# An edge layer regrouped: partitions of four m quarters times 32 channels, sums in 128x32 products, VectorE's second operand in PSUM

## The chip, the cores and the metric

The kernel runs on one NeuronCore of a Trainium2 chip. The metric is the device time of one execution in microseconds (us), as the median of several runs. One further execution was recorded by the hardware profiler. All times inside the kernel come from that one.

The engines are called by the profile's names: PE is TensorE (PEld its weight loads), DVE is VectorE, ACT is ScalarE, POOL is GpSimd and SP is the engine that issues most DMAs. SBUF is the working memory and PSUM the memory that PE writes to, in eight banks of 512 float32 values in each of 128 partitions.

## The reference

The input x has shape (4, 56, 56, 128). Four layers are computed, each as `x = x + layer(groupnorm(x))`: a windowed attention layer, an edge layer, a spectral attention layer and a convolution. The change lies in the second one only:

```
# x: (b, l, n, f), all of 4 images, 56 rows l, 56 columns n, 128 channels f
W1, W2 = We[:, :f], We[:, f:]
proj_i = einsum('blnf,of->blno', x, W1)
proj_j = einsum('blnf,of->blno', x, W2)
edge = relu(proj_i[:, :, :, None, :] + proj_j[:, :, None, :, :] + be)
edge_sum = edge.sum(axis=3)                       # over the 56 columns m of the same row
node_in = concatenate([x, edge_sum], axis=-1)
node = relu(einsum('blnc,oc->blno', node_in, Wn) + bn)
```

For every row l and every pair of columns (n, m) of that row there is a relu over 128 channels, summed over m. That is 56 x 56 x 56 x 128 relu terms for an image.

## The kernel before, in words

**Around the edge layer.** `build` treats the four images in turn (`first_layers`): a fast form of the windowed layer (lines below L1140), then `edge_layer` (L1150), then a store. In the measured runs, the branch `small` is taken. Only when the edge layer of the fourth image has ended do the spectra, the attention and the outputs of the later layers begin. The first work of the next stage (POOL's memsets at L339, VectorE's normalization at L193) follows the last `finish` of the edge layer, because its pools take over the space.

**How the edge layer is tiled.** Channels lie on the 128 partitions. An image's 3136 pixels are cut into NBLK = 7 blocks of NB = 448 pixels, that is 8 rows of 56. For one block j:

- `project(j)` (L1181): two products of 128x128 with 448 columns, `pc` = W2 x (L1184) and `pa` = W1 x (L1186), each into a PSUM bank.
- `evacuate(j)` (L1189): ScalarE writes c = -(pc + be) to SBUF (L1194), copies pa to a (L1196), and adds bn to x in place (L1197).
- The relu of a + pc + be is written as max(a, c) - c. Fourteen turns, given by the string `EDGE_TURNS = "ddpddpdpddpddp"` (L1147), handle four values of m each. In a "d" turn (nine of them) VectorE computes max(pa, c) for 4 x 448 values per partition into a tile `e_td` (L1231). It reads pa from PSUM, repeated four times, and c from SBUF, repeated along n. In a "p" turn (five) GpSimd computes a - c into `e_tp` (L1233) and ScalarE applies relu to it in place (L1235).
- After each turn PE sums (L1238): 16 products of a 32x32 identity block with 32 channels of one m. Output partitions are the quarter q of the m, banks are the channel group r, so `acc` has four banks, in which (q, channel of r) are the partitions.
- The correction for the "d" turns is the sum of c over their m, `e_rest`, by one VectorE reduction (L1248).
- At the end of the block ScalarE copies the four banks of acc to `e_sums` (L1250, 128x1792). Then `output` of the block before (L1200) makes six products of 448 columns into the bank `po`: one of x (L1202), one of rest (L1203) and four of sums (L1206). `project(j + 2)` follows.
- `finish(j - 2, po)` (L1211), called in turn 3 of the next block, is one VectorE instruction that takes po from PSUM, applies the last relu and adds to x.

**What sets the order.** Inside `tc.manual_schedule` the instructions of PE, ScalarE and VectorE run in the order in which the Python loop writes them. GpSimd's queue holds only the "p" turns here. Semaphores tie the engines together. A turn's tile comes from a pool of seven ("d") or four ("p"), so VectorE may run up to seven "d" tiles ahead of PE. All eight PSUM banks are used: acc 4, pa 2, and pc and po share 2.

Of the kernel before, what the change touches and what calls it, by code (L numbers as in the profile page):

```python
# [19 lines left out]
P = 128  # L20
# [1129 lines left out]
def edge_layer(k, w, x1, st):  # L1150

    nc, tc = k.nc, k.tc
    xf = x1.rearrange("p l n -> p (l n)")
    nd = 4 * EDGE_TURNS.count("d")
    quarters = [slice(32 * q, 32 * q + 32) for q in range(4)]
    with ExitStack() as es:  # L1160
        big = es.enter_context(tc.tile_pool(name="e_big", bufs=1))
        wk = es.enter_context(tc.tile_pool(name="e_wk", bufs=2))
        psum = es.enter_context(tc.tile_pool(name="e_ps", bufs=2, space=PSUM))

        def bank():
            return psum.tile([P, 512], F32, tag="mm", name="e_mm")

        mr = group_norm_factors(k, wk, bank, st)
        xg = big.tile([P, TOK], F32, name="e_xg")
        shift = wk.tile([P, 1], F32, name="e_shift", bufs=1)  # L1170
        nc.vector.tensor_scalar(shift, mr[:, 0:1], mr[:, 1:2], -1.0, ALU.mult, ALU.mult)
        ready = {}

        def normed(j):
            if j < 2:
                apply_norm(k, xg[:, blk(j)], xf[:, blk(j)], mr)
            elif j < NBLK:
                nc.scalar.activation(xg[:, blk(j)], xf[:, blk(j)], AF.Identity, bias=shift, scale=mr[:, 1:2])

        def project(j):  # L1180
            if j >= NBLK:  # L1181
                return
            pc = psum.tile([P, 512], F32, tag="mm", name="e_pc")
            nc.tensor.matmul(pc[:, :NB], w.W2, xg[:, blk(j)], start=True, stop=True)  # L1184
            pa = psum.tile([P, 512], F32, tag="pa", name="e_pa")
            nc.tensor.matmul(pa[:, :NB], w.W1, xg[:, blk(j)], start=True, stop=True)  # L1186
            ready[j] = pa, pc

        def evacuate(j):  # L1189
            if j >= NBLK:  # L1190
                return
            pa, pc = ready[j]
            c = wk.tile([P, 8, HH], F32, name="e_c")
            nc.scalar.activation(c.rearrange("p l m -> p (l m)"), pc[:, :NB], AF.Identity, bias=w.nbe, scale=-1.0)  # L1194
            a = wk.tile([P, NB], F32, name="e_a")
            nc.scalar.copy(a, pa[:, :NB])  # L1196
            nc.scalar.activation(xf[:, blk(j)], xf[:, blk(j)], AF.Identity, bias=w.bn)  # L1197
            ready[j] = pa, a, c

        def output(j, rest, sums):  # L1200
            po = psum.tile([P, 512], F32, tag="mm", name="e_po")
            nc.tensor.matmul(po[:, :NB], w.Wn[:, 0, :], xg[:, blk(j)], start=True, stop=False)  # L1202
            nc.tensor.matmul(po[:, :NB].rearrange("p (l n) -> p l n", l=8), w.nWn, bc(rest, 2, HH),  # L1203
                             start=False, stop=False)
            for r in range(4):
                nc.tensor.matmul(po[:, :NB], w.Wnq[:, r, :], sums[:, r, :], start=False, stop=(r == 3))  # L1206
            return po

        def finish(j, po):

            nc.vector.scalar_tensor_tensor(xf[:, blk(j)], po[:, :NB], w.nbn, xf[:, blk(j)], ALU.max, ALU.add)  # L1211

        with tc.manual_schedule(engines={mybir.EngineType.PE, mybir.EngineType.Activation, mybir.EngineType.DVE}):
            for j in range(2):
                normed(j)
            for j in range(2):
                project(j)
                evacuate(j)
            last = po = None
            for j in range(NBLK):  # L1220
                pa, a, c = ready.pop(j)
                acc = psum.tile([P, 4, 512], F32, name="e_acc", bufs=1)
                rest = wk.tile([P, 8], F32, name="e_rest")
                at = {"d": 0, "p": nd}
                for g, e in enumerate(EDGE_TURNS):
                    t = wk.tile([P, 4, 8, HH], F32, tag="e_" + e, name="e_t" + e, bufs=7 if e == "d" else 4)
                    cm = bc(c[:, :, at[e]:at[e] + 4].rearrange("p l m -> p m l"), 3, HH)
                    at[e] += 4
                    if e == "d":
                        am = bc(pa[:, :NB].rearrange("p (l n) -> p l n", l=8), 1, 4)  # L1230
                        nc.vector.tensor_tensor(t, am, cm, ALU.max)  # L1231
                    else:
                        nc.gpsimd.tensor_sub(t, bc(a.rearrange("p (l n) -> p l n", l=8), 1, 4), cm)  # L1233
                        tf = t.rearrange("p m l n -> p (m l n)")
                        nc.scalar.activation(tf, tf, AF.Relu)  # L1235
                    for q in range(4):
                        for r, o in enumerate(quarters):
                            nc.tensor.matmul(acc[quarters[q], r, :NB], k.ident[o, o],  # L1238
                                             t[o, q].rearrange("p l n -> p (l n)"),
                                             start=(g == 0), stop=(g == len(EDGE_TURNS) - 1))  # L1240
                    if g == 3 and po is not None:
                        finish(j - 2, po)
                    if g == 5 and j:
                        evacuate(j + 1)
                    if g == 8:
                        normed(j + 2)
                    if g == 9:
                        nc.vector.tensor_reduce(rest, c[:, :, 0:nd], AX.X, ALU.add)  # L1248
                sums = wk.tile([P, 4, NB], F32, name="e_sums")
                nc.scalar.copy(sums, acc[:, :, :NB])  # L1250
                if last:
                    po = output(*last)
                project(j + 2)
                last = j, rest, sums
            finish(NBLK - 2, po)
            finish(NBLK - 1, output(*last))


def edge_weights(k, w, pool):

    for n, t in (("nbe", w.be), ("nbn", w.bn), ("nWn", w.Wn[:, 1, :])):
        r = pool.tile(list(t.shape), F32, name="e_" + n)
        k.nc.vector.tensor_scalar_mul(r, t, -1.0)
        setattr(w, n, r)


def l1_host(i):
    We, Wn = i["L1_conv_We"], i["L1_conv_Wn"]
    W2 = Wn[:, P:].T.reshape(4, 1, 32, P)
    return {  # L1270
        "w1_W1": We[:, :P].T, "w1_W2": We[:, P:].T, "w1_be": i["L1_conv_be"].reshape(P, 1),
        "w1_Wn": Wn.T.reshape(2, P, P).transpose(1, 0, 2), "w1_bn": i["L1_conv_bn"].reshape(P, 1),
        "w1_Wnq": np.broadcast_to(W2, (4, 4, 32, P)).reshape(4, P, P).transpose(1, 0, 2),
    }


# [1564 lines left out]
```

## Time and profile before

| what | value |
|---|---|
| time, median of 3 runs | 3583.2 us (3579.53 to 3584.5) |
| the profiled execution's own time | 3579.81 us |
| its span, first to last instruction | 3578.0 us |
| mean granted TensorE clock | 0.981 |
| PE busy, share of the span | 3372.0 us, 94% |
| DVE busy | 2702.3 us, 76% |
| ACT busy | 2089.9 us, 58% |
| POOL busy | 1249.2 us, 35% |
| edge layer of the four images, from its first normalization to its last finish | 150.46, 150.50, 150.50 and 150.70 us |

A page of the profile gives the busy time of each engine, the groups of instructions (source line, engine, operation, tile written and tiles read, shapes, count, busy time and mean duration), and the chain of work that ended last. The shares above are means over stages that have different limits, so what one stage is worth is read from that stage alone. Two views serve for this: the table of engine busy times in chosen windows, and the timeline, which merges neighbouring instructions of one kind and shows in brackets how long an engine sat idle before them and what it waited for. A PE product in float32 is recorded as two weight loads and two matmul instructions, so counts of PE instructions are twice the products in the code. Ends of matmuls are modelled: a run of them is better read from start to start.

### The profile page before, as it was taken

The numbers are of one execution on the slowest core, as the hardware profiler recorded it, in microseconds if no ns is written. First come the engines' busy times: TensorE is split into PE (matmuls) and PEld (weight loads), VectorE is DVE, ScalarE is ACT, GpSimd is POOL, SyncE is SP. The second block draws the span as 40 slices with busy tenths as digits, with TensorE's granted clock in tenths as the row PEclk, the third lists the DMA queues.
The fourth block names the chain that finished last, engine by engine and source line by source line (L and its number), as shares of the span: only waits on it lengthen the run. The fifth ranks groups of instructions, "written<-read, shape, count | busy, mean of one in ns | idle before, by whom it ended". The sixth has DMA issues, their size and how long they took to land.

```text
span 3578.0 us, 80873 instructions
## 1 busy us (share of the span) xinstructions
PE 3372.0 (94%) x36096; PEld 1549.4 (43%) x36096; DVE 2702.3 (76%) x2531; ACT 2089.9 (58%) x2103; POOL 1249.2 (35%) x752
## 2 busy tenths in 40 slices
PE   6999998989999898999999999999898899999998
PEld 4433344553333455333344643333456443336664
DVE  6588868767888696688859758887784678886776
ACT  4688865458888564688856458887552112214442
POOL 1000017600000581000018400000673778884686
PEclk8999999999999999999999999999998999999999
DMA  2144420014333000444310024442103027763101
GB/s 103 43 92 92 95 42 20 20 47 94 88 88 83 20 3 20 99 93 94 89 44 3 20 57 94 94 94 63 38 3 101 15 53 178 181 148 91 55 19 55
DMA packets 98076, 244.51 MB, mean 68 GB/s; under 512 B 64456, under 2 KB 69832, under 8 KB 92712
## 3 DMA queue, kind: packets, MB, share of 16 engines
q0 software_dynamic: 16128, 102.77, 14.2%
q1 hardware_dynamic: 74872, 123.64, 11.9%
q10 hardware_dynamic: 6720, 12.85, 1.3%
q8 instruction: 285, 4.67, 0.5%
q14 instruction: 71, 0.58, 0.1%
HBM read 79.46 MB, written 31.33 MB: 31 GB/s over the span
## 4 chain that ended last, share of the span: by engine, by line
PE 79%; DVE 10%; ACT 4%; issue 4%; POOL 3%; DMA 0%; POOLq 0%; DVEq 0%; ACTq 0%
PE f_pm L818 17%; PE f_pm L684 15%; PE u_po L1878 8%; PE e_acc L1238 7%; PE q_acc L1732 3%; DVE e_td L1231 3%; PE f_pm L791 2%; PE e_po L1206 2%; PE f_pm L770 2%; ACT f_ring L821 1%; PE f_pm L464 1%; PE o_d L2141 1%; DVE f_acc L673 1%; PE o_d L2538 1%; PE f_pm L715 1%
## 5 line engine op out<-in xcount | busy, mean ns | idle before, releaser
L821 ACT ACTIVATE f_ring<-f_pm 128x1792 f32<-128x1792 f32 (+1 forms) x764 | 1093.8, 1482 | 228.7 <-PE f_pm L818 181.2
L673 DVE TENSOR_TENSOR f_acc<-f_acc,f_ring 128x1792 f32<-128x1792 f32 x468 | 947.7, 2025 | 191.1 <-ACT f_ring L821 160.9
L818 PE MATMUL f_pm<-f_qT,f_kT 32*128 32x448 f32 x5376 | 725.2, 571 | 15.5 <-ACT f_ring L821 5.1
L684 PE MATMUL f_pm<-f_ring,f_va 128*32 128x448 f32 (+1 forms) x6304 | 589.4, 490 | 0.0
L663 POOL DMA_DIRECT2D f_far<-f_ring x112 | 96.6, 862 | 1329.3 <-ACT f_ring L821 1108.2
L1231 DVE TENSOR_TENSOR e_td<-e_pa,e_c 128x1792 f32<-128x1792 f32 x252 | 491.2, 2018 | 14.1 <-ACT e_a L1196 14.1
L1233 POOL TENSOR_TENSOR e_tp<-e_a,e_c 128x1792 f32<-128x1792 f32 x140 | 451.5, 3261 | 101.4 <-PE e_acc L1238 59.8
L818 PEld LDWEIGHTS f_pm<-f_qT,f_kT 32*128 32x128 f32 x5376 | 260.4, 183 | 417.2 <-ACT f_ring L821 304.7
L1238 PE MATMUL e_acc<-e_td,t_shared 32*32 32x448 f32 x8064 | 325.8, 545 | 24.9 <-DVE e_td L1231 24.0
L684 PEld LDWEIGHTS f_pm<-f_ring,f_va 128*32 128x32 f32 x6304 | 164.2, 109 | 409.7 <-issue 397.4
L1873 DVE TENSOR_TENSOR u_ud<-u_px,u_d 112x1792 f32<-112x1792 f32 x144 | 263.5, 1864 | 39.6 <-PE u_po L1878 35.4
L1235 ACT ACTIVATE e_tp<-e_tp 128x1792 f32<-128x1792 f32 x140 | 233.4, 1694 | 74.0 <-POOL e_tp L1233 74.0
L1875 POOL TENSOR_TENSOR u_up<-xh,u_d 112x1792 f32<-112x1792 f32 (+1 forms) x72 | 240.9, 3376 | 55.0 <-PE u_po L1878 39.7
L1238 PE MATMUL e_acc<-e_tp,t_shared 32*32 32x448 f32 x4480 | 222.6, 544 | 3.0 <-ACT e_tp L1235 2.4
L1878 PE MATMUL u_po<-u_ud,AT 112*64 112x448 f32 x1056 | 213.8, 544 | 1.9 <-DVE u_ud L1873 1.9
L1238 PEld LDWEIGHTS e_acc<-e_td,t_shared 32*32 32x32 f32 x8064 | 142.3, 103 | 138.4 <-DVE e_td L1231 79.4
L1878 PEld LDWEIGHTS u_po<-u_ud,AT 112*64 112x64 f32 x1056 | 74.4, 138 | 128.8 <-issue 112.9
L1250 ACT COPY e_sums<-e_acc 128x1792 f32<-128x1792 f32 x28 | 46.3, 1652 | 136.2 <-PE e_acc L1238 136.2
L1238 PEld LDWEIGHTS e_acc<-e_tp,t_shared 32*32 32x32 f32 x4480 | 96.5, 103 | 53.0 <-issue 16.6
L728 DVE RECIPROCAL f_den<-f_den 128x448 f32<-128x448 f32 x28 | 82.6, 2951 | 44.1 <-ACT f_den L725 44.1
L1717 POOL TENSOR_TENSOR q_u<-iS,q_g 128x1792 f32<-128x1792 f32 x32 | 102.8, 3236 | 23.0 <-PE q_acc L1732 22.8
L1732 PE MATMUL q_acc<-q_u,S 64*64 64x448 f32 x1024 | 104.6, 553 | 4.4 <-DVE q_u L1719 3.3
(525 smaller groups left out, 4511.6 us busy)
## 6 DMA issues: line engine op xcount, KB each, us to landing
f_far<-f_ring POOLq DMA_DIRECT2D x112, 896.0 KB, 6.3
u_d<-dd SPq DMA_DIRECT2D x46, 784.0 KB
f_far<-f_ring SPq DMA_DIRECT2D x28, 896.0 KB
xw<-in_x SPq DMA_DIRECT2D x4, 1568.0 KB
x2d<-x SPq DMA_DIRECT2D x4, 1568.0 KB
xat<-x SPq DMA_DIRECT2D x4, 1568.0 KB
x_xs<-xat ACTq DMA_DIRECT2D x32, 196.0 KB
xm<-x_ev ACTq DMA_DIRECT2D x64, 98.0 KB
```

Source lines behind the costliest of these rows:

```text
L673: nc.vector.tensor_add(e.acc, e.acc, slots(j, c))
L684: nc.tensor.matmul(e.po[heads[h], part], va[o, c, heads[h]], p, start=(c == 0), stop=(c == 23 and part.stop == NB))
L818: nc.tensor.matmul(ss[:, i, :NB], kT[heads[h], c * P:(c + 1) * P], qT[heads[h], blk(j)], start=True, stop=True)
L821: nc.scalar.activation(ring[:, slot:slot + m, :], ss[:, :m, :NB], AF.Exp, scale=scale)
L1231: nc.vector.tensor_tensor(t, am, cm, ALU.max)
L1233: nc.gpsimd.tensor_sub(t, bc(a.rearrange("p (l n) -> p l n", l=8), 1, 4), cm)
L1235: nc.scalar.activation(tf, tf, AF.Relu)
L1238: nc.tensor.matmul(acc[quarters[q], r, :NB], k.ident[o, o], t[o, q].rearrange("p l n -> p (l n)"), start=(g == 0), stop=(g == len(EDGE_TUR ...
L1732: nc.tensor.matmul(acc[bp][i][halves[hb % 2], hb // 2, :NB], x[o], u[o, 8 * hb:8 * hb + 8, :].rearrange("p h t -> p (h t)"), start=first, ...
L1873: nc.vector.tensor_mul(u, bc(px[:, :, :NB], 2, m), dm)
L1875: nc.gpsimd.tensor_mul(u, bc(x, 2, m), dm)
L1878: nc.tensor.matmul(po[64 * b2:64 * b2 + 64, :NB], st.AT[:, 8 * i + h0 + q, 2 * bp + b2, :], u[:, b2, q, :], start=(left == 16), stop=(left ...
```

## The change

Instead of the 128 channels of one m at a time, a tile now carries, on its partitions, four quarters of the m (m = 14 q + i) times 32 channels, and, along its free axis, the four channel groups r. A turn handles the four m values with the same i.

- `project` makes four products for pa, one for each r, with the 32 channels of W1 repeated four times (weights from the host), into four single banks. For pc it makes 16 products of 128x32 with 112 columns, with -W2, which put the 14 m values of a quarter q into partition range q.
- `evacuate` is split in two parts, after turns 5 and 7. ScalarE moves the four pa banks to SBUF, with be added (`e_a`, 4 x 448), and pc to `e_c`. Block 1's evacuation moves from ahead of the loop into block 0.
- A "d" turn reads `e_a` from SBUF as its first operand and pc from PSUM, repeated along n, as its second. A "p" turn reads `e_a` and `e_c` from SBUF. The tile is 128x1792 as before. In block 0 the first three "d" turns and the first "p" turn are cut into four pieces, one for each r.
- PE sums a turn in four products of 128x32, one for each r, with a stack of four 32x32 identities, into the four partition ranges of one bank `acc`. Partitions of acc are now the channels.
- Four more such products subtract rest (128x4x8 now) inside acc. `e_sums` becomes 128x448, and `output` two products: x and sums.
- Banks: pa 4, pc 2, acc 1, and one for po and the normalization's small products.
- On the host: the packed weights hold W1 four times, a stack of identities and its negative; the four-times-wide Wn for sums and its negated copy go.

`EDGE_TURNS` stays as it is; the new turn letter "s" that the code knows doesn't occur in it. The diff, cut to its core:

```diff
         def project(j):
             if j >= NBLK:
                 return
-            pc = psum.tile([P, 512], F32, tag="mm", name="e_pc")
-            nc.tensor.matmul(pc[:, :NB], w.W2, xg[:, blk(j)], start=True, stop=True)
-            pa = psum.tile([P, 512], F32, tag="pa", name="e_pa")
-            nc.tensor.matmul(pa[:, :NB], w.W1, xg[:, blk(j)], start=True, stop=True)
-            ready[j] = pa, pc
-
-        def evacuate(j):
+            pa = [psum.tile([P, 512], F32, name="e_pa", bufs=4) for r in range(4)]
+            pc = psum.tile([P, 512], F32, name="e_pc", bufs=2)
+
+            def first(r):
+                nc.tensor.matmul(pa[r][:, :NB], w.W1[:, r, :], xg[:, blk(j)], start=True, stop=True)
+            first(0)
+            xm = xg[:, blk(j)].rearrange("p (l m) -> p l m", l=8)
+            for r, o in enumerate(quarters):
+                for q in range(4):
+                    nc.tensor.matmul(pc[quarters[q], 8 * M * r:8 * M * (r + 1)].rearrange("p (l m) -> p l m", l=8),
+                                     w.nW2[:, o], xm[:, :, M * q:M * (q + 1)], start=True, stop=True)
+            for r in range(1, 4):
+                first(r)
...
+        def evacuate(j, part):
...
-            c = wk.tile([P, 8, HH], F32, name="e_c")
-            nc.scalar.activation(c.rearrange("p l m -> p (l m)"), pc[:, :NB], AF.Identity, bias=w.nbe, scale=-1.0)
-            a = wk.tile([P, NB], F32, name="e_a")
-            nc.scalar.copy(a, pa[:, :NB])
-            nc.scalar.activation(xf[:, blk(j)], xf[:, blk(j)], AF.Identity, bias=w.bn)
...
+            for r in range(2 * part, 2 * part + 2):
+                nc.scalar.activation(a[:, r, :], pa[r][:, :NB], AF.Identity, bias=w.be[:, r:r + 1])
+                if r == 0:
+                    nc.scalar.copy(c.rearrange("p r l m -> p (r l m)"), pc[:, :NB])
+            if part == 1:
+                nc.scalar.activation(xf[:, blk(j)], xf[:, blk(j)], AF.Identity, bias=w.bn)
+
+        def terms(j, m, t, r0, r1, e):
+            pc, _, c, a = ready[j]
+            if e == "d":
+                c = pc[:, :NB].rearrange("p (r l m) -> p r l m", r=4, l=8)
+            cm = bc(c[:, r0:r1, :, m], 3, HH)
+            am = a[:, r0:r1, :].rearrange("p r (l n) -> p r l n", l=8)
+            if e == "d":
+                nc.vector.tensor_tensor(t, am, cm, ALU.max)
+            else:
+                nc.gpsimd.tensor_sub(t, am, cm)
+                tf = t.rearrange("p r l n -> p (r l n)")
+                nc.scalar.activation(tf, tf, AF.Relu)
...
             po = psum.tile([P, 512], F32, tag="mm", name="e_po")
             nc.tensor.matmul(po[:, :NB], w.Wn[:, 0, :], xg[:, blk(j)], start=True, stop=False)
-            nc.tensor.matmul(po[:, :NB].rearrange("p (l n) -> p l n", l=8), w.nWn, bc(rest, 2, HH),
-                             start=False, stop=False)
-            for r in range(4):
-                nc.tensor.matmul(po[:, :NB], w.Wnq[:, r, :], sums[:, r, :], start=False, stop=(r == 3))
+            nc.tensor.matmul(po[:, :NB], w.Wn[:, 1, :], sums, start=False, stop=True)
...
-            for j in range(2):
-                project(j)
-                evacuate(j)
+            project(0)
+            for part in range(2):
+                evacuate(0, part)
+            project(1)
...
+                if j == 0:
+                    early = {g: tile_of(EDGE_TURNS[g]) for g in
+                             [g for g, e in enumerate(EDGE_TURNS) if e == "d"][:3] + [EDGE_TURNS.index("p")]}
+                    for r in range(4):
+                        for g, t in early.items():
+                            terms(j, ms[g], t[:, r:r + 1], r, r + 1, EDGE_TURNS[g])
...
-                    for q in range(4):
-                        for r, o in enumerate(quarters):
-                            nc.tensor.matmul(acc[quarters[q], r, :NB], k.ident[o, o],
-                                             t[o, q].rearrange("p l n -> p (l n)"),
-                                             start=(g == 0), stop=(g == len(EDGE_TURNS) - 1))
+                    for t, r0 in parts:
+                        for r in range(t.shape[1]):
+                            nc.tensor.matmul(acc[quarters[r0 + r], :NB], w.S[:, 0, :], t[:, r].rearrange("p l n -> p (l n)"),
+                                             start=(g == 0), stop=False)
                     if g == 3 and po is not None:
                         finish(j - 2, po)
-                    if g == 5 and j:
-                        evacuate(j + 1)
+                    if g == 5:
+                        evacuate(j + 1, 0)
+                    if g == 7:
+                        evacuate(j + 1, 1)
+                    if g == 10:
+                        normed(j + 2)
                     if g == 8:
-                        normed(j + 2)
-                    if g == 9:
-                        nc.vector.tensor_reduce(rest, c[:, :, 0:nd], AX.X, ALU.add)
-                sums = wk.tile([P, 4, NB], F32, name="e_sums")
-                nc.scalar.copy(sums, acc[:, :, :NB])
+                        if ns:
+                            nc.vector.tensor_reduce(rest[:, 0:2], ready[j][2][:, 0:2, :, 0:nd + 1], AX.X, ALU.add)
+                        nc.vector.tensor_reduce(rest[:, 2 if ns else 0:4], ready[j][2][:, 2 if ns else 0:4, :, 0:nd], AX.X, ALU.add)
+                for r in range(4):
+                    nc.tensor.matmul(acc[quarters[r], :NB].rearrange("p (l n) -> p l n", l=8), w.S[:, 1, :],
+                                     bc(rest[:, r, :], 2, HH), start=False, stop=True)
+                sums = wk.tile([P, NB], F32, name="e_sums")
+                nc.scalar.copy(sums, acc[:, :NB])
                 if last:
                     po = output(*last)
                 project(j + 2)
```

## The prediction

> **What bounds the kernel now.** I read the page first, then, for the edge layer alone, the table of engine busy times in windows, the chain of waits, and the timelines of VectorE and PE. The page gives the groups that the edit touches:
>
> ```profile
> L1231 DVE TENSOR_TENSOR e_td<-e_pa,e_c 128x1792 f32<-128x1792 f32 x252 | 491.2, 2018 | 14.1 <-ACT e_a L1196 14.1
> L1233 POOL TENSOR_TENSOR e_tp<-e_a,e_c 128x1792 f32<-128x1792 f32 x140 | 451.5, 3261 | 101.4 <-PE e_acc L1238 59.8
> ```
>
> VectorE's turns (252 = 28 blocks x 9) never wait inside a block; GpSimd waits for PE (to get a tile back). The windows of two successive blocks of the first image, from finish to finish, show why:
>
> ```profile
> core 0: us, PE busy (x) PEld busy (x) DVE busy (x) ACT busy (x) POOL busy (x), PEclk, DMA share, GB/s
> 615.84:635.52 19.68, 19.68 (x465) 11.71 (x464) 18.42 (x12) 12.09 (x11) 16.13 (x6) 1.00 0.01 2
> 635.52:655.20 19.68, 19.68 (x465) 11.70 (x464) 18.42 (x11) 12.09 (x11) 16.14 (x6) 1.00 0.01 3
> ```
>
> The first number is the block's length, then each engine's busy time. PE is busy for all 19.68 us, VectorE for 18.42. The chain of waits over such a block is PE alone:
>
> ```profile
> 597.62 13.47 PE e_acc L1238 x437
> 611.09 0.95 PE e_po L1202 x2
> 612.04 0.75 PE e_po L1203 x2
> 612.79 3.01 PE e_po L1206 x8
> 615.80 0.75 PE e_pc L1184 x2
> 616.55 0.75 PE e_pa L1186 x2
> ```
>
> So 14 turns of sums take 13.47 us, 0.962 a turn, and eight full products of 448 columns 6.21, that is 0.75 each and 0.2 for the change of array mode. VectorE pays for PE at each finish:
>
> ```profile
> 604.84 9.74 DVE L1231 TENSOR_TENSOR e_td<-e_pa,e_c 128x1792 f32<-128x1792 f32 x5
> 615.84 0.69 DVE L1211 SCALAR_TENSOR_TENSOR x<-e_po,e_nbn,x 128x448 f32<-128x448 f32 x1 [1.26 <-PE e_po L1206]
> ...
> 683.57 3.95 DVE L1231 TENSOR_TENSOR e_td<-e_pa,e_c 128x1792 f32<-128x1792 f32 x2
> 694.45 0.68 DVE L1211 SCALAR_TENSOR_TENSOR x<-e_po,e_nbn,x 128x448 f32<-128x448 f32 x1 [6.93 <-PE e_po L1206]
> 699.03 0.68 DVE L1211 SCALAR_TENSOR_TENSOR x<-e_po,e_nbn,x 128x448 f32<-128x448 f32 x1 [3.89 <-PE e_po L1206]
> ```
>
> Blocks 2 to 6 each hold a finish that waits (1.14, then four times 1.26: 6.18 us an image), and after the last VectorE turn (687.52) PE needs another 11.5 us until the last finish starts. From the five turns in 9.74 us with 2.02 for one, turns follow each other every 1.93 to 1.94 us.
>
> **What the Trainium skill says.** "TensorEngine Tiling (Array Packing)", Available Configurations, lists 128x32 as four independent tiles, and Key Properties says that changing the mode drains the engine. The trace agrees: the 0.2 us above, and these lines from the attention of the first layer, where 128x32 products write the four partition ranges of one bank:
>
> ```profile
> 1053.46 0.96 PE L684 MATMUL f_pm<-f_ring,f_va 128*32 128x448 f32 x8
> ...
> 1056.70 0.96 PE L715 MATMUL f_pm<-f_acc,c_ones 128*32 128x448 f32 x8
> ```
>
> Eight instructions (four products) read 0.96; a run of 16 of L684 reads 1.71, so four products take 0.75 in a stream, as one full product does. "VectorE: DVE Perf Modes", The perf-mode tier table, gives float32 tensor_tensor one rate whether operands are in SBUF or PSUM. The trace agrees: 2018 ns with the first operand in PSUM, 2025 (L673) with both in SBUF, 1549 for 1344 elements with the second in PSUM (L761), all about 1.04 ns an element plus 150. "SBUF — State Buffer", Who interferes with whom: a VectorE instruction with at most one SBUF input doesn't contend with GpSimd, one with two does. Before and after have one; before, GpSimd's turns stay within 3245 to 3279 ns beside VectorE. That stands for "after" too, but no line here has the new operand arrangement.
>
> **The change part by part, for a block.**
>
> PE, sums: 14 turns x 0.75 = 10.5 in place of 13.47. PE, output: two products, 1.5, in place of six, 4.5. PE, rest inside acc: four 128x32 products, 0.75 (the product of the spread rest, L1203, ran at 0.75, so repeated columns cost nothing). PE, pa: 4 x 0.75 = 3.0 in place of 0.75. PE, pc: 16 products of 112 columns. If four overlap, 4 x 0.75/4 = 0.75; by the issue pace of the 32x32 turns (0.962/32 = 0.030 an instruction) 32 x 0.030 = 0.96; without any overlap 16 x 0.75/4 = 3.0. I take 0.96, since eight 128x32 instructions overlap in the lines above, and keep 0.75 and 3.0 as ends. Mode changes: four a block (into output, into pc, out of it, into sums) x 0.2 = 0.8. Sum: 10.5 + 1.5 + 0.75 + 3.0 + 0.96 + 0.8 = 17.5 in place of 19.68 (ends 17.3 and 19.6).
>
> VectorE: nine turns x 1.94, a reduction of 288 elements (0.36 start to start) and a finish (0.60): 18.42, unchanged. The turn's cost is the one thing that no row shows in its new form. Lower end: 1792 elements at 1.04 ns are 1.87, 0.07 less a turn; upper end: the accumulating adds of L673 follow each other every 2.13 when they don't wait (three in 6.29), 0.19 more. I take 1.94: two L761 products of 1344 and 448 elements, 1.549 + 0.612 long, take 2.09 together at 1156.74, so an instruction with its second operand in PSUM also overlaps its successor by 0.07.
>
> So VectorE becomes the bound at 18.42, and PE's 0.9 of slack covers its own share. Is finish then free of its wait? After the last turn of a block PE has one or two turns (0.75 each), rest (0.75) and output (1.5) to do: po is there some 4 us after VectorE's last turn. VectorE does three turns (5.8 us) before finish, so the wait goes. PE comes to sums again after project, some 8.5 us in, with four or five of the seven "d" tiles full, so VectorE doesn't stop for a tile either.
>
> ScalarE: five relus x 1.70, evacuation of four pa banks 4 x 0.6, of pc 0.53, x 0.68, xg 0.75, sums 0.53 in place of 1.65: some 13.4, in place of 12.09, within 18.42. Its queue matters at the split evacuation only: part 0 stands behind the relu of turn 5, part 1 behind that of 7, and neither is needed before the next block. If that cover were gone, each microsecond late would delay GpSimd's first tile, which itself is four tiles ahead. GpSimd: 5 x 3.23 = 16.1, unchanged, within 18.42. No DMA is moved; the packed weights are about as large as before.
>
> Start of the image: now the first turn starts 4.4 us after the normalization (549.24 to 553.64). After: pa 0 at the slow early pace (the next product's first instruction at 551.45 follows those two of 549.80 by 1.65, some 0.8 an instruction), to 551.3, pc by 552.9 to 553.4, ScalarE's copy of pc (0.53) until some 553.9: +0.3. The copy and VectorE read the same bank, and the first turn of before likewise started only when ScalarE had left pa's bank (3.48 us idle, until L1196). Then twelve pieces of 448 elements, 0.54 start to start (L729 to L738) = 6.5 in place of three turns, 5.8: +0.7. ScalarE and PE supply pieces every 0.75, less than the 1.6 that VectorE needs for three. Project(1) on PE is over by some 560, when the first tiles are full.
>
> End of the image: from VectorE's last turn, before, 687.52 to 699.71, 12.2. After: one turn's sums 0.75 + 0.14, turn 13 0.75, rest 0.75: 2.4. Output of block 5, 1.5, to 3.9. The one po bank makes output of block 6 wait for finish of 5 (0.69, to 4.9), then 1.5, and finish to 7.35. That is 4.8 less.
>
> Sum for an image: 6.18 + 4.8 - 0.3 - 0.7 = 10.0. Nothing else runs beside the edge layer's end: the next stage's first VectorE and GpSimd work (699.13, 699.63) follows the last finish, after all four images. So 4 x 10.0 = 40 us. Against the profiled execution's own 3579.8 that gives 3539.8; the median of the runs shown stands 3.4 above it, so 3543.
>
> **The rivals.** First: pc doesn't overlap, and PE stays the bound at 19.0 to 19.6. For it: strided reading of 14 columns at a time, of which no row shows a case; against it: L684's pace. Then finish's wait shrinks only by 0.1 to 0.7 in five blocks, the end by 4.8: 4 x (2 + 4.8 - 1.5) = 21: 3562.
>
> Second, slower: VectorE's turns lose their overlap and follow every 2.13. For it: L673's chain, and an operand order not seen before; against it: L761, and that L673 reads its own output. Price: 60 whole turns and 12 pieces an image, 72 x 0.19 = 13.7, x 4 = 55, less 40: 15 slower, 3598. It decides from 40/288 = 0.14 us an instruction. Third: the four sums of a turn don't overlap, against L684 and L715: 14 x 3.0 = 42 us a block, over 800 us slower. Fourth: VectorE's turn gets 0.07 cheaper, with a PE that just follows (17.5): 252 x 0.07 = 18 more: 3525.
>
> **How the numbers follow.** Forecast 0.70 (3534 to 3552), PE still the bound 0.12 (3552 to 3570), VectorE's overlap lost 0.10 (3577 to 3600), cheaper turns 0.05 (3523 to 3534), sums without overlap 0.03. Range 3530 to 3566: it leaves out the last two, the slower case and the rims. About 0.2% (7 us) is what a measurement of this kernel can tell from no change. Faster by more: 0.70 + 0.12 + 0.05 = 0.87, less 0.01 at the rim; same 0.03; slower 0.11.
>
> **What would show it.** Right: in the windows from finish to finish 18.4 us, VectorE busy all of it, PE some 17; no wait for e_po before finish in blocks 2 to 6; the e_td mean at 2018; 56 + 4 sum products a block at 0.75 per four; from last turn to last finish 7 to 8 us; edge layer some 140.5 us in place of 150.5. Wrong: e_td longer than 2.02 or spaced by more than 2.0, VectorE waiting for PE inside a block, pc above 2 us a block, or GpSimd's mean well above 3261.

## The result, and the profile after

| | before | after |
|---|---|---|
| median of the timed runs, us | 3581.8 (4 runs, 3579.5 to 3584.5) | 3539.5 (4 runs, 3534.4 to 3542.2) |
| ratio to before, 95% interval | 1 | 0.988 (0.9863 to 0.9897) |
| profiled execution, its span, us | 3579.8, 3578.0 | 3540.0, 3538.2 |
| edge layers of the four images, us | 150.6, 150.6, 151.5, 150.8: 603.5 | 140.1, 140.0, 140.2, 140.4: 560.8 |
| all the rest of the span, us | 2974.5 | 2977.4 |

An edge layer is counted here from the start of the write of e_shift, VectorE's first instruction after the normalization's statistics, to the end of the last finish, both from VectorE's timeline. (The table of the profile before has 150.50 for the third image; counted as there it is 151.34.) The gain lies there: 42.7 us less in the profiled executions, with 2.9 given back outside. The groups of the page that answer to those of before (the changed kernel has other line numbers):

```profile
L1222 DVE TENSOR_TENSOR e_td<-e_a,e_pc 128x1792 f32<-128x1792 f32 (+1 forms) x288 | 493.3, 1781 | 15.3 <-ACT e_c L1210 15.1
L1224 POOL TENSOR_TENSOR e_tp<-e_a,e_c 128x1792 f32<-128x1792 f32 (+1 forms) x152 | 453.7, 3023 | 75.1 <-issue 43.2
L1277 PE MATMUL e_acc<-e_td,t_edge 128*32 128x448 f32 x2016 | 225.4, 543 | 42.4 <-DVE e_td L1222 42.4
```

The means of 1781 and 3023 ns mix whole turns with pieces of 448 elements; VectorE's busy time in the group, 493.3 us, was 491.2 before. What has turned round is the last line: PE now idles 42.4 us for tiles of VectorE, where before it was busy in the whole block. The windows of two blocks of the first image, from finish to finish, columns as before:

```profile
core 0: us, PE busy (x) PEld busy (x) DVE busy (x) ACT busy (x) POOL busy (x), PEclk, DMA share, GB/s
616.03:634.36 18.33, 17.43 (x172) 6.50 (x164) 18.33 (x12) 12.32 (x14) 16.15 (x6) 1.00 0.00 1
634.36:652.69 18.33, 17.43 (x172) 6.51 (x164) 18.33 (x12) 12.32 (x14) 16.15 (x6) 1.00 0.01 2
```

VectorE is busy for the whole block of 18.33 us, PE for 17.43. The chain of waits over one block, which was PE alone before, now passes from PE to VectorE and back:

```profile
614.53 0.75 PE e_pa L1190 x2
615.28 0.90 PE e_pc L1195 x32
616.19 2.45 PE e_pa L1190 x6
618.64 3.19 PE e_acc L1277 x32
...
622.41 0.23 DVE e_rest L1290
622.64 0.14 issue
622.78 5.88 DVE e_td L1222 x3
628.66 0.04 issue
628.70 1.71 PE e_acc L1277 x16
630.41 0.75 PE e_acc L1292 x8
631.16 0.95 PE e_po L1234 x2
632.11 0.75 PE e_po L1235 x2
```

Four products of the rest take 0.75 (L1292), the output 1.70 in two products with its change of mode, the sixteen products of pc 0.90 (32 instructions), and four sum groups 3.19. VectorE's timeline shows the start, a finish inside the layer and the end:

```profile
555.83 12.26 DVE L1222 TENSOR_TENSOR e_td<-e_a,e_pc 128x448 f32<-128x448 f32 x15 [3.78 <-ACT e_c L1210]
...
616.03 0.68 DVE L1240 SCALAR_TENSOR_TENSOR x<-e_po,e_nbn,x 128x448 f32<-128x448 f32 x1
616.62 5.87 DVE L1222 TENSOR_TENSOR e_td<-e_a,e_pc 128x1792 f32<-128x1792 f32 x3
...
677.78 5.87 DVE L1222 TENSOR_TENSOR e_td<-e_a,e_pc 128x1792 f32<-128x1792 f32 x3
687.90 0.68 DVE L1240 SCALAR_TENSOR_TENSOR x<-e_po,e_nbn,x 128x448 f32<-128x448 f32 x1 [4.26 <-PE e_po L1235]
690.45 0.68 DVE L1240 SCALAR_TENSOR_TENSOR x<-e_po,e_nbn,x 128x448 f32<-128x448 f32 x1 [1.86 <-PE e_po L1235]
```

The finish at 616.03 has no bracket: it waits for nothing, where the finish at the same place waited 1.26 before. From the last turn's end (683.65) to the last finish's end (691.13) are 7.48 us, 12.2 before.

### The profile page after: what moved, and what is told of

It reads as the page before. It is cut to its first block, busy times and chain, and to the rows that moved or that the text cites. A ratio compares the mean times of both kernels' runs of the same rounds, so it can differ in the third digit from the quotient of the medians.

```text
span 3538.2 us, 64217 instructions
## 1 busy us (share of the span) xinstructions
PE 3317.8 (94%) x27696; PEld 1429.6 (40%) x27696; DVE 2694.3 (76%) x2566; ACT 2102.1 (59%) x2199; POOL 1251.9 (35%) x764
## 4 chain that ended last, share of the span: by engine, by line
PE 75%; DVE 15%; ACT 4%; issue 3%; POOL 2%; DMA 0%; DVEq 0%; POOLq 0%; ACTq 0%; SPq 0%
PE f_pm L818 18%; PE f_pm L684 15%; PE u_po L1924 8%; DVE e_td L1222 7%; PE q_acc L1778 3%; PE e_acc L1277 3%; PE f_pm L791 2%; PE f_pm L770 2%; PE e_pa L1190 2%; ACT f_ring L821 1%; PE o_d L2584 1%; PE f_pm L464 1%; PE s_pr L1573 1%; PE o_d L2187 1%; DVE f_acc L673 1%
## 5 line engine op out<-in xcount | busy, mean ns | idle before, releaser
L684 PE MATMUL f_pm<-f_ring,f_va 128*32 128x448 f32 (+1 forms) x6304 | 591.0, 491 | 0.0
L1222 DVE TENSOR_TENSOR e_td<-e_a,e_pc 128x1792 f32<-128x1792 f32 (+1 forms) x288 | 493.3, 1781 | 15.3 <-ACT e_c L1210 15.1
L1224 POOL TENSOR_TENSOR e_tp<-e_a,e_c 128x1792 f32<-128x1792 f32 (+1 forms) x152 | 453.7, 3023 | 75.1 <-issue 43.2
L684 PEld LDWEIGHTS f_pm<-f_ring,f_va 128*32 128x32 f32 x6304 | 163.9, 109 | 410.7 <-issue 398.4
L1277 PE MATMUL e_acc<-e_td,t_edge 128*32 128x448 f32 x2016 | 225.4, 543 | 42.4 <-DVE e_td L1222 42.4
L1226 ACT ACTIVATE e_tp<-e_tp 128x1792 f32<-128x1792 f32 (+1 forms) x152 | 236.9, 1583 | 45.3 <-POOL e_tp L1224 44.9
L1277 PE MATMUL e_acc<-e_tp,t_edge 128*32 128x448 f32 x1120 | 131.0, 540 | 3.3 <-ACT e_tp L1226 3.1
L1277 PEld LDWEIGHTS e_acc<-e_td,t_edge 128*32 128x32 f32 x2016 | 55.5, 109 | 191.0 <-DVE e_td L1222 115.3
L1924 PE MATMUL u_po<-u_up,AT 112*64 112x448 f32 x480 | 103.9, 546 | 2.4 <-POOL u_up L1921 2.4
L1190 PE MATMUL e_pa<-e_xg,t_edge 128*128 128x448 f32 x224 | 101.1, 578 | 5.1 <-DVE e_xg L193 5.1
```

The lines of the kernel that those rows point to most:

```text
L684: nc.tensor.matmul(e.po[heads[h], part], va[o, c, heads[h]], p, start=(c == 0), stop=(c == 23 and part.stop == NB))
L1224: nc.gpsimd.tensor_sub(t, am, cm)
L1277: nc.tensor.matmul(acc[quarters[r0 + r], :NB], w.S[:, 0, :], t[:, r].rearrange("p l n -> p (l n)"), start=(g == 0), stop=False)
L1924: nc.tensor.matmul(po[64 * b2:64 * b2 + 64, :NB], st.AT[:, 8 * i + h0 + q, 2 * bp + b2, :], u[:, b2, q, :], start=(left == 16), stop=(left ...
```

## Experiments

My theory was the prediction's: PE was the bound, the change takes PE below VectorE, and from there VectorE sets the block. Its rivals were that the gain came from elsewhere (VectorE's new operand, the new start), or that PE is still in the way. The table gives each kernel's time and, from its profile, the sum of the four edge layers and one block of the first image. Two kernels with the same code outside the edge layer differ by up to 16.5 us there (half_turn_room and no_pieces), so a difference of a few microseconds is read from the edge layers and not from the total.

| kernel | median us | ratio to before (95%) | edge layers | block | PE, VectorE, GpSimd busy in it |
|---|---|---|---|---|---|
| after | 3539.5 | 0.988 (0.9863 to 0.9897) | 560.8 | 18.33 | 17.43, 18.33, 16.15 |
| after_again | 3544.2 | 0.9888 (0.9873 to 0.9903) | 561.1 | | |
| before_one_sum | 3530.6 | 0.9866 (0.9849 to 0.9882) | 557.9 | 18.33 | 17.66, 18.33, 16.40 |
| both_in_sbuf | 3956.2 | 1.1059 (1.1041 to 1.1078) | 979.8 | 33.30 | 21.99, 33.30, 22.05 |
| pc_serial | 3546.6 | 0.991 (0.9893 to 0.9926) | 567.1 | 18.33 | 18.33, 18.33, 16.03 |
| pe_plus_1 | 3547.4 | 0.9896 (0.9881 to 0.9911) | 560.6 | 18.33 | 18.18, 18.33, 16.14 |
| pe_plus_4 | 3572.7 | 0.9982 (0.9975 to 0.9988) | 590.0 | 20.23 | 20.23, 18.42, 16.16 |
| no_pieces | 3556.1 | 0.9923 (0.9909 to 0.9936) | 569.6 | | |
| last_bank | 3535.3 | 0.9866 (0.9851 to 0.9881) | 556.7 | | |
| half_turn | 3541.1 | 0.9893 (0.9877 to 0.991) | 555.7 | 17.78 | 17.64, 17.53, 17.78 |
| half_turn_and_bank | 3543.6 | 0.9892 (0.9877 to 0.9907) | 552.5 | | |
| spare_products | 3548.2 | 0.9907 (0.9893 to 0.992) | 561.0 | | |
| half_turn_room | 3530.9 | 0.9852 (0.9838 to 0.9865) | 550.5 | 17.79 | 17.64, 17.53, 17.79 |

**Was PE the bound before?** In the kernel before, three of the output's four products with the sums are left out; nothing else of it changes.

```diff
-            for r in range(4):
+            for r in range(3, 4):
                 nc.tensor.matmul(po[:, :NB], w.Wnq[:, r, :], sums[:, r, :], start=False, stop=(r == 3))
```

> The kernel before, with one of the four products of sums in output; three quarters of the edge sums are left out of the result. Theory (PE bounds a block before): PE 19.68 - 3 x 0.75 = 17.43 us a block, below VectorE's 18.42, so the finish no longer waits (6.2 us an image) and the end of an image shrinks by two outputs, 4.5: 4 x 10.7 = 43 less, 3539 us, though nothing else of the change is in. Rival (the gain comes from the new operands or the new order): only the end shrinks, 4 x 4.5 = 18 less, 3564.

Measured: 3530.6 us, and this block:

```profile
613.48:631.81 18.33, 17.66 (x460) 10.06 (x458) 18.33 (x13) 11.87 (x11) 16.40 (x6) 1.00 0.01 3
```

With some 2 us less on PE and VectorE's operands, layout and start untouched, the block falls to the same 18.33 us as in the changed kernel, with VectorE busy in all of it, and the edge layers lose 45.6 us. That is all of the changed kernel's gain in the edge layers and a little more (the start stays as it was). So the gain is PE's relief; the new operands and layout are the way to it.

**What VectorE's second operand in PSUM is worth.** VectorE's turns read e_c, the copy in SBUF that GpSimd reads anyway.

```diff
-            if e == "d":
-                c = pc[:, :NB].rearrange("p (r l m) -> p r l m", r=4, l=8)
```

> The changed kernel, but VectorE's turns take their second operand from the copy of pc in SBUF, so both come from SBUF, beside GpSimd's turns. Theory (two SBUF inputs contend with GpSimd): if they exclude one another, a block takes 17.4 + 16.2 = 33.6 us in place of 18.33, some 430 us more in all; if GpSimd alone is stretched, up to its slack of 2.2 us a block is hidden; I expect at least 3600. Rival (float32 operands cost the same wherever they lie, also beside GpSimd): 3540, e_td at 2.02 and e_tp at 3.26.

Measured: 3956.2 us. The table of one block, and in a second fence the two groups of turns by tile (min/median/max in ns, pieces of 448 elements included, then first and last start):

```profile
639.75:673.05 33.30, 21.99 (x165) 6.54 (x164) 33.30 (x13) 11.91 (x13) 22.05 (x5) 0.74 0.00 0
```

```profile
L1220 DVE TENSOR_TENSOR e_td<-e_a,e_c x288: 610/2014/5084, 555.7 to 3051.4; 128x1792 f32<-128x1792 f32 x120, 128x448 f32<-128x448 f32 x24
L1222 POOL TENSOR_TENSOR e_tp<-e_a,e_c x152: 1202/4641/5172, 555.8 to 3038.2; 128x1792 f32<-128x1792 f32 x136, 128x448 f32<-128x448 f32 x16
```

The turns of the two engines exclude each other. Of VectorE's 240 whole turns, 116 still take 2.0 us, but the other 124 take 4.6 to 5.08, which is nearly one turn of its own (2.02) and one of GpSimd (3.26 when undisturbed), and GpSimd's reach 5.17. (The medians in the fence mix both kinds with the pieces.) The wait for the other engine counts as busy time in the longer instruction, so no idle column shows it: VectorE reads 33.30 us busy out of 33.30 for work of 18.33. The reckoning from full exclusion, 33.6 us a block and 430 more in all, stands against 33.30 and 416.7 measured. The Trainium skill, "SBUF — State Buffer", Who interferes with whom, has the rule (a VectorE instruction with two SBUF inputs contends with a GpSimd instruction that reads SBUF); these runs agree and give the size. GpSimd reads both its operands from SBUF, so the operand in PSUM isn't a detail of the change: without it the change would cost 374 us against before.

**Does the order of the pc products matter?** Two loops exchanged, so that four successive products write the same partition range.

```diff
-            for r, o in enumerate(quarters):
-                for q in range(4):
+            for q in range(4):
+                for r, o in enumerate(quarters):
```

> The changed kernel, with the 16 products of pc in the other order: four successive ones write the same partition range. Theory (the overlap over the four ranges is what makes them cheap): pc takes up to 3.0 us in place of 0.90, PE up to 19.5 us a block, above VectorE's 18.33; five blocks an image longer by 1.2 and the start later by 2: 4 x 8 = 32 more, 3572. Rival (pc runs at the issue pace in any order, 0.03 an instruction): 0.9 to 1.0, 3540.

Measured: 3546.6 us. From the chain and from the table of one block:

```profile
615.14 2.13 PE e_pc L1195 x32
```

```profile
615.77:634.10 18.33, 18.33 (x166) 7.75 (x164) 18.33 (x12) 12.42 (x14) 16.03 (x6) 1.00 0.00 1
```

Neither side was right: the sixteen products take 2.13 us in place of 0.90, so the order counts, but not the 3.0 of a stream without any overlap. PE's 18.33 then just fits VectorE's block, which stays; the 6.3 us more in the edge layers are the starts, where pc is on the path. In the four images the first turn comes 6.9, 5.9, 6.0 and 7.0 us after e_shift, and 4.7 to 4.9 in the changed kernel: 6.6 more in all. The exchange has a second effect that no run separates from the first: four successive products shared their weights before it, and share their columns of x after it.

**How much slack has PE?** A product of the first projections is repeated, once and four times, from the third block of an image on, and writes the same values again.

```diff
+            for n in range(1 if j > 1 else 0):
+                first(3)
```

and with 4 for 1.

> The changed kernel with one product of project made twice, in the five projects inside the blocks (0.75 us of PE each). Theory (0.9 us of slack a block): PE 18.18 a block, still below VectorE's 18.33, nothing is lost, 3540 (at most 3 more). Rival (no slack): 20 x 0.75 = 15 more, 3555.

> The changed kernel with the last product of project made five times instead of once, in the five projects inside the blocks (3.0 us of PE each). Theory (PE has 0.9 us of slack a block): each of those blocks grows by 3.0 - 0.9 = 2.1, 5 x 4 x 2.1 = 42 more, 3581, which is the time before. Rival (no slack, all on the path): 20 x 3.0 = 60 more, 3600.

Measured, one block of each:

```profile
618.13:636.46 18.33, 18.18 (x174) 6.93 (x166) 18.33 (x13) 12.32 (x14) 16.14 (x6) 1.00 0.01 1
```

```profile
615.61:635.84 20.23, 20.23 (x173) 8.16 (x172) 18.42 (x12) 12.44 (x14) 16.16 (x6) 1.00 0.01 2
```

One product (0.75) disappears: block 18.33, edge layers 560.6 against 560.8 (the total's excess over the changed kernel lies outside of them). Four bring the old picture back, PE busy throughout, VectorE at 18.42, and the wait ahead of finish, here in VectorE's timeline:

```profile
635.84 0.68 DVE L1242 SCALAR_TENSOR_TENSOR x<-e_po,e_nbn,x 128x448 f32<-128x448 f32 x1 [1.81 <-PE e_po L1237]
```

The edge layers lose 7.3 us an image, where I had reckoned 10.5. A late block is only 1.90 longer (20.23 less 18.33), not 2.1: PE's own work in the changed kernel is then 20.23 less 3.0, or 17.23, and its slack nearer to 1.1 than to 0.9. And only four blocks of an image pay. Of the five finishes inside the layer of the first image the first doesn't wait at all, the second waits 1.35 and the others 1.81; they stand 19.75 and three times 20.23 apart. The likely reason, not tested by itself, is a lead of the engines that the first late projects use up.

**Do the twelve pieces of the first block earn their place?** The branch for the first block is switched off; its turns are whole and wait for the whole evacuation.

```diff
-                if j == 0:
+                if j < 0:
```

> The changed kernel with whole turns in block 0, too. The first turn then waits for all four evacuations of pa, which ended 2.9 us after the first turn's start in the changed kernel; the twelve pieces took 0.65 more than three whole turns. Theory (VectorE is the bound from its first turn on): 4 x (2.9 - 0.65) = 9 more, 3549. Rival (PE comes late to the first sums anyway, and a later start is hidden): 3540.

Measured: 3556.1 us, edge layers 569.6: 8.8 more, 2.2 an image. VectorE's timeline (e_shift was written at 553.27):

```profile
560.61 11.68 DVE L1222 TENSOR_TENSOR e_td<-e_a,e_pc 128x1792 f32<-128x1792 f32 x6 [6.29 <-ACT e_a L1208]
```

The first turn starts 7.3 us after e_shift, 2.5 later than in the changed kernel, and in the other images 2.2 to 3.9 later: 11.5 in all. Less the 0.65 an image that whole turns save, 8.9 are left, about what the edge layers lost. The four pa banks, PE's 3.0 us in place of 0.75, would lie on the start if the turns weren't cut.

**What limits the changed kernel now: the end and VectorE.** Two edits, each alone. The last output of an image goes to the bank of pc, which nobody uses then:

```diff
-            po = psum.tile([P, 512], F32, tag="mm", name="e_po")
+            po = psum.tile([P, 512], F32, tag="e_pc" if j == NBLK - 1 else "mm", name="e_po",
+                           bufs=2 if j == NBLK - 1 else 1)
```

> The changed kernel, with the last output of an image written to the free bank of pc instead of the one po bank. Theory: its products no longer wait for the finish before (PE sat idle 0.8 to 0.9 us there): 4 x 0.9 = 3.6 less, 3536; from the last turn to the last finish's end 6.6 in place of 7.5. Rival (the copy of sums would hold it anyway): 3540.

Measured: 3535.3 us, the best until then; edge layers 556.7, 1.0 less an image. The two finishes at the end, in VectorE's timeline:

```profile
675.40 5.87 DVE L1222 TENSOR_TENSOR e_td<-e_a,e_pc 128x1792 f32<-128x1792 f32 x3
685.52 0.68 DVE L1241 SCALAR_TENSOR_TENSOR x<-e_po,e_nbn,x 128x448 f32<-128x448 f32 x1 [4.26 <-PE e_po L1236]
687.03 0.68 DVE L1241 SCALAR_TENSOR_TENSOR x<-e_po,e_nbn,x 128x448 f32<-128x448 f32 x1 [0.82 <-PE e_po L1236]
```

They start 1.51 us apart in place of 2.55, and the end takes 6.45 us in place of 7.48. The output of block 6 does wait for the finish of 5 in the changed kernel, as the prediction's sum for the end had it.

The other edit gives half of one of VectorE's turns in a block to GpSimd ("s" is a turn in two halves, one for each):

```diff
-EDGE_TURNS = "ddpddpdpddpddp"
+EDGE_TURNS = "ddpddpspddpddp"
```

> The changed kernel with one of the nine VectorE turns shared: two channel groups on VectorE, two on GpSimd. Theory (VectorE is now the bound, at 18.33, with PE at 17.43 and GpSimd at 16.15): VectorE 17.5, GpSimd 17.9, PE 17.5 with no room; a block takes some 17.9, 28 x 0.43 = 12 less, 3528. Rival (with three engines this near to each other, waits of one for the other eat it): 3540 or more.

Measured: 3541.1 us, one block:

```profile
613.35:631.13 17.78, 17.64 (x165) 6.45 (x164) 17.53 (x12) 13.38 (x15) 17.78 (x7) 1.00 0.00 1
```

GpSimd is the bound at 17.78, with PE 0.14 and VectorE 0.25 behind it. The edge layers gain 5.1 us, not the 12 expected: the end takes 9.28 instead of 7.48, and finish waits again, 1.25 to 2.11 the first time in an image and about 0.26 from then on. And the total gains nothing: the stretch after the fourth edge layer takes 897.3 us in place of 892.0. I put both edits together, to see whether they add up:

> The changed kernel with the shared turn and with the last output in pc's free bank. The shared turn alone made a block 17.78 us (GpSimd busy all of it) and the four edge layers 555.7 in place of 560.8; the bank alone 556.7. Theory: the two add up, edge layers 551.5 to 552, 9 us less than the changed kernel, 3530. Rival (with the shared turn PE is later at the image's end, so that the bank is free in time anyway): 555, 3535.

Measured: 3543.6 us. The edge layers do add up (552.5), the total doesn't: the last stretch is now 902.9. The first difference to look at is the loads of s_x, which the attention stage behind it reads. The same line in the changed kernel:

```profile
2497.24 1.98 SPq L2827 DMA_DIRECT2D s_x<-xad  x4
```

and in half_turn:

```profile
2638.79 2.56 SPq L2827 DMA_DIRECT2D s_x<-xad  x4
```

They go out at 2497 us ahead of the fourth edge layer in the one, and at its very end in the other, where PE then waits 4.89 us for them (5.11 in half_turn_and_bank). That wait is not itself what costs the time: the changed kernel has waits of 2.83 and 2.56 at the same place, and PE gets to the next step (s_ps) 15.9 us after the last finish in half_turn and 17.2 in the changed kernel. half_turn falls behind later, at a VectorE instruction on one element a partition. In half_turn and in the changed kernel:

```profile
2678.33 7.73 DVE L1505 SCALAR_TENSOR_TENSOR s_t<-s_t,s_mv 128x1 f32<-128x1 f32 x1
```

```profile
2689.77 0.23 DVE L1505 SCALAR_TENSOR_TENSOR s_t<-s_t,s_mv 128x1 f32<-128x1 f32 x1
```

PE waits 9.13 us for it in half_turn, 1.83 in the changed kernel. In half_turn_and_bank the instruction before it (L1505 there) takes 7.12. Their inputs lie in SBUF, and GpSimd works without a pause beside them, on weights whose loads now stand behind those of s_x in the queue: it first touches them (t_w_qk) 19.4 us after the last finish, in place of 2.1. So this looks like the exclusion of both_in_sbuf, met by way of the order of the loads; no run tests that link by itself. A theory for the loads themselves: the extra half tiles take the room in SBUF that s_x had. The last kernel makes that room, with one buffer for each half tile in place of two, and six in place of seven for VectorE's whole ones, which is as much as the changed kernel takes:

```diff
-                            bufs=2 if n < 4 else 7 if e == "d" else 4)
+                            bufs=1 if n < 4 else 6 if e == "d" else 4)
```

> The changed kernel with both edits of half_turn_and_bank (the last full GpSimd tile of a block changed into two halves, one for each engine; the last output of an image written into the convolution's PSUM bank), and with SBUF room made for them: one buffer instead of more for each of the four half tiles, six instead of eight for VectorE's full tiles. Nothing of the computation is left out. My theory of why half_turn_and_bank gained 8.6 us in the edge layers and nothing in the total: its extra half tiles took the SBUF room of s_x, so that s_x's loads went out only after the fourth edge layer (at 2635 us) and TensorE waited 4.9 to 5.1 us for them there. Then here s_x's loads go out before the fourth edge layer as in the changed kernel (near 2500 us), the stretch after it is 890 to 893 us instead of 902.9, the edge layers stay at 552 to 553 us, and the total is some 8 us below the changed kernel's: 3530 to 3533. The rival: the loads were not what cost the time, the stretch stays at 897 to 903 us and the total at 3540 or more. A third outcome: six tiles are too few for VectorE, which then shows waits on TensorE inside a block and edge layers of over 560 us.

(There were seven whole tiles before, not eight; the shared turn is one of VectorE's, as in half_turn, and the bank is pc's.) Measured: 3530.9 us, and in the queue:

```profile
2489.96 2.07 SPq L2828 DMA_DIRECT2D s_x<-xad  x4
```

The loads are early again, the last stretch takes 888.0 us in place of 902.9, the edge layers 550.5, and six tiles are enough for VectorE. So the room decided when the loads go out. What they cost is less sure: in the kernels that load s_x early the stretch lies anywhere from 887.2 (before) to 898.4 (pe_plus_4), half_turn's 897.3 is within that, and only half_turn_and_bank's 902.9 is outside. This is a version that beats both kernels: 0.9852 (0.9838 to 0.9865) against 0.988 (0.9863 to 0.9897) and 0.9888 (0.9873 to 0.9903) of the two measurements of the changed kernel. The first two intervals just touch; the edge layers' 10.3 us less are the surer evidence. Against last_bank (0.9866) the times don't separate, only the edge layers (550.5 and 556.7).

**What comes back after the fourth edge layer.** In the changed kernel, the stretch from there to the end takes 892.0 us, 887.2 before. PE's first products there, before and after:

```profile
2691.04 6.22 PE L1527 MATMUL s_pr<-t_images,s_x 128*64 128x33 f32 x207 [1.00 <-PE e_po L1206]
2700.51 1.07 PE L1527 MATMUL s_pr<-t_images,s_x 128*64 128x33 f32 x17 [3.24 <-issue]
```

```profile
2648.31 4.09 PE L1573 MATMUL s_pr<-t_images,s_x 128*64 128x33 f32 x81 [2.83 <-DMA t_w_qk<-in_w_qk]
...
2654.96 7.74 PE L1573 MATMUL s_pr<-t_images,s_x 128*64 128x33 f32 x143 [2.56 <-issue]
```

PE stands idle for 2.83 and 2.56 us where it stood for 1.00 and 3.24, which is 1.15 more. PE is also slower in between: 207 instructions take 6.22 us before, at a granted clock of 1.00, and 81 take 4.09 after, where it was 0.57 (2649 to 2652 us). The changed kernel was run once more, and beside it with twenty spare products of 128 columns after the last output of the fourth image, to see whether work on PE right behind the edge layer shortens the stretch:

```diff
+            if extra:
+                spare = psum.tile([P, 512], F32, tag="e_acc", name="e_spare")
+                for n in range(extra):
+                    nc.tensor.matmul(spare[:, :P], k.ident, k.ident, start=True, stop=True)
```

> The changed kernel once more, as a measure for the two runs beside it and of how far the stages outside the edge layer vary by themselves. Theory: edge layers 560.8 us in all, to 0.5; the stretch after the fourth edge layer 892 us, since PE's next products start 4.5 to 5 us after PE's last wait in the edge layer in every kernel with little PE work left there; 1.2% less than before. Rival (that stretch varies by chance): some 887 as before, or 897.

> The changed kernel with 20 spare products of 128 columns (0.21 us each, 4.3 in all, constants only, result not used) after the last output of the fourth image. They need no wait, so PE's queue gets past them to the next part of the program while PE is still busy. Theory (what comes after the edge layer waits for the instructions of the next part to arrive, and PE's clock falls in that wait): PE's next products start right after the spare ones, some 3 us after the last finish, at full clock, and the stretch after the fourth edge layer shrinks from 892 to some 888: 4 less, 3536. Rival (PE waits there for data, or for the clock whatever it does): 892 or more, 3540 to 3543.

Measured: after_again 3544.2 us with a last stretch of 891.8, as in the first run; spare_products 3548.2, with 894.0. PE runs the spare products from 2650.4 to 2655.1 and then idles for 2.64 and again for 3.93 us. So my theory fell, and the cause of these gaps stays open. (half_turn_room, with the stretch at 888.0, still shows 2.20 for the DMA and 2.02 for issue.)

## Why the prediction was right, point by point

**PE's sum.** 17.5 forecast, 17.43 measured. The 0.75 for four overlapping 128x32 products held in the sums, in the rest and, nearly, in pc (0.96 taken, 0.90 measured). What I hadn't seen is that pc's pace depends on its loops going round the four partition ranges: exchanged, the products cost 2.13. Taking the pace from L684 was right only together with L684's order, and the sum didn't ask about the order: that it fitted is luck.

**VectorE as the new bound.** 18.42 forecast, 18.33 measured. The starts in the timeline are 1.93 us apart (six turns from 622.78 to the finish at 634.36), so nine turns are 17.37; a reduction is 0.37 and a finish 0.59, in all 18.33. The one unknown, the turn with its second operand in PSUM, is as dear as the old one (2014 ns median for whole turns, 2018 before). The 0.09 too much are 9 x 0.01 of the spacing. No finish inside the layer waits any more, and the pe_plus runs bracket PE's slack: 0.75 more is free, 3.0 more isn't, and the block of pe_plus_4 puts it at 1.1.

**GpSimd and ScalarE.** GpSimd 16.15 for 16.1: it was not slowed, and both_in_sbuf shows that this rested on the operand in PSUM. ScalarE 12.32 for 13.4: a relu is 1.70 long, as taken, but the sum added full lengths, and neighbours overlap by about 0.1 (two relus together read 3.29). It had no consequence, as ScalarE isn't the bound.

**Start and end.** The first turn starts 4.70 us after the normalization of x, 4.40 before: +0.3 as forecast. The twelve pieces and three turns take 12.26 (6.5 and 5.8 were reckoned). The end is 7.48 for 7.35, and last_bank confirms the term in it for the shared bank.

**The sum.** 10.0 us an image forecast, 42.7/4 = 10.7 measured. Half of the 0.7 is the overlap that a finish gets back when it no longer waits: 0.09 for each of five, 0.45. Some 0.2 more is the third image of the kernel before, whose edge layer took 0.6 to 0.9 longer than the other three. Outside the edge layer I had counted nothing; the profiled execution gives back 2.9 net, 4.8 of it in the stretch after the fourth edge layer, with 1.9 gained elsewhere. So the forecast of 40 (39.8 measured in the profiled executions, 42.2 between the medians) came out so close by luck in part: a gain a little larger than forecast met a small loss that I hadn't foreseen.

**The rivals.** PE still the bound: no, by 0.9 us a block or a little more; with the other loop order it is level, at 18.33 and not at 19.0 to 19.6. Overlap of VectorE's turns lost: no (1.93). Sums without overlap: no. Cheaper turns: no.

## What to carry to other kernels

When the bound engine is relieved, the gain ends where the next engine stands, and that can be read beforehand from a window of one block: here 19.68 to 18.4, although PE lost more than that. Before moving an operand, see which engine reads SBUF beside it: one operand in PSUM or two in SBUF were 18.3 or 33.3 us a block, and the loss shows as longer instructions, not as waiting. And when an edit adds tiles, look at the loads of the stages behind it: the half tiles, with two buffers for each kind, put s_x's loads off by 140 us, and the two kernels that had them gained nothing in the total from a faster edge layer.

## What the runs showed of the hardware

- Exclusion between VectorE and GpSimd when both read two operands from SBUF: instructions of 2.02 and 3.26 us grew to as much as 5.08 and 5.17, and the block, 33.30, nearly to the sum of both engines' turns.
- Sixteen products of 112 columns in 128x32 form took 0.90 us when successive ones wrote different partition ranges, 2.13 when four in a row wrote the same one, at the same granted clock of 1.00.
- A wait of VectorE for PE costs a little more than its length: turns are 2.02 long but 1.93 apart, and a finish that waits loses that overlap with the turn ahead of it (a wait of 1.26 made the block 1.35 longer, 19.68 for 18.33).
- After the fourth edge layer PE idles for no reason that the profile shows, 3.24 us before, 2.56 in the changed kernel, and 2.64 and 3.93 behind the spare products. Its granted clock is at 0.50 for some 15 us in the changed kernel and for 6 before. Neither is explained here.
